# A graph network of two layers on one core: group 1's input loaded early into a tile of another pool, and the timetable of its steps changed

## Chip, cores, metric

One core of one Trainium2 chip. The metric is the device time of one execution in microseconds (us); medians of several executions are quoted. All executions used here are in the fast state; the mean granted TensorE clock of the profiled ones lies between 0.988 and 0.992 of full speed.

## The reference, cut to what matters

128 graphs of 128 nodes with 256 features pass two layers. `adj` is a 128x128 matrix of integers for each graph.

```python
# layer 0: two graph attentions in a row, then a feed-forward part
Wh = h @ W;  e = leaky_relu(Wh @ a[:F] + (Wh @ a[F:]).T, 0.2)
att = softmax(where(adj > 0, e, -9e15), axis=1)
h = att @ Wh                                     # done twice (W1, a1; W2, a2)
h = layernorm(x + h)
x = layernorm(h + relu(h @ w_ff1) @ w_ff2)
# layer 1: attention with 8 heads and 4 relations, then a feed-forward part
attn = softmax(q @ k.T / sqrt(32))
out = sum over r of (attn * (adj == r)) @ (x @ Wv[r])
x = layernorm(x + out @ Wo)
x = layernorm(x + gelu(x @ W1) @ W2)
```

## The kernel before

The kernel takes four graphs as a group; there are 32 groups, counted from 0. Each of the five stages of a group (load, graph attention "gat", feed-forward 0, attention, feed-forward 1) is a Python generator. A generator emits some instructions and yields a distance. A heap merges the generators of all groups by time, so the numbers in `TIMES`, `EARLY` and `stages` are a timetable that decides in which order PE's instructions (and, by the scheduler, those of the other engines) stand. They are no waits.

```python
TIMES = {
    "sums": 5, "ff unit": 3, "ff2": 4, "ff half": 10, "row": 13, "gat": 18, "wh": 5.5,
    "gat copy": 0, "qk": 4.5, "scores": 5, "turn0": 10, "turn1": 5,
    "v0": 5.5, "mask0": 0, "av": 6.5, "v": 3.5, "mask": 3,
    "end": 1, "lead ff0": 26, "lead att": 32, "lead ff1": 32, "affine": 6, "store": 25,
}
...
def load_group(g):                                # xT and mask of a group
    xt = ld.tile([P, DC, T], F32, name="xt", bufs=1)
    nc.sync.dma_start(xt, xT[g])
    return xt, load_mask(g)
...
def unit(f0):                                     # in feed_forward: one half of the first product
    ...
    product(chain, 1, True); product(side, 5, True)            # product: L300
    nc.scalar.copy(lo[:, :, 0], chain); nc.scalar.copy(hi[:, :, 1], side)
    yield
    ...
    nc.vector.tensor_add(lo[:, :, 1], lo[:, :, 1], side)       # L315
    yield
    product(chain, 7)
    nc.vector.tensor_add(hi[:, :, 1], hi[:, :, 1], chain)      # L318
    yield
    product(chain, 4)                             # L300 again: writes the same PSUM tile, so it waits for L318
    for i in range(2):
        nc.scalar.activation(lo[:, i], lo[:, i], func, ...)    # L322
    for i in range(2):
        nc.scalar.activation(hi[:, i, 1], ...)                 # L325
        nc.scalar.activation(hi[:, i, 0], chain[:, i], ...)    # L326: gives the PSUM tile back
    yield
...
def gat_weighting(wh, c, cap, direct):            # the softmax of one graph attention
    ...                                           # not direct: the row goes out and back through DRAM
        nc.vector.transpose(z, ...)                            # L359, zs
        nc.sync.dma_start(s.rearrange(...), z[::Q])            # L361, zsd <- zs
        nc.sync.dma_start(p, ...)                              # L363, e <- zsd
    yield TIMES["row"]
    ...                                           # Prelu L366, cap L367, max L369, exp L372, 1/s L373
    nc.gpsimd.tensor_mul(e, e, per_row(s, N))                  # L374
    return e

def gat_block(direct, tag, g, xt, at):
    ...                                           # wh = x W, L385
    att = yield from gat_weighting(wh, D + 2, cap, direct)
    yield TIMES["gat"]
    ...                                           # first att @ wh, L393; copies L394
    yield TIMES["gat copy"]
    nc.sync.dma_start(y, x[g])                                 # tok
    att = yield from gat_weighting(wh, D, cap, direct)
    yield TIMES["gat"]
    ...                                           # second att @ wh, L403
...
# attention: weights(b) = scores L438, max L444, exp L448, scaling L450; turned = transpose L249 or
# through DRAM L255 to L260; by_relation = mask L464; values L471, L472; weighted = av product L483
    yield TIMES["qk"]
    es = [weights(0)]
    yield TIMES["scores"]
    es.append(weights(1))
    ...
    yield TIMES["v0"]
    v, ms = values(0), {}
    for k in range(0, 8, 2):
        by_relation(0, eT[0], ms, PARTS[k // 2:k // 2 + 1])
        yield TIMES["mask0"]
    for b in range(G):
        ...
        yield TIMES["av"]
        oT, last = weighted(ms, v)
...
stages = (stage_load, -81), (stage_gat, -39), (stage_ff0, 48), (stage_attention, 132), (stage_ff1, 300)
```

The second product after the softmax, the output projection, is L521; the second matrix of the feed-forward part is L343.

## Time and profile before

| | kernel before |
|---|---|
| time, median (range, runs) | 3256.7 us (3255.5 to 3259.5, 4) |
| profiled span | 3254.6 us |
| PE busy | 3137.8 us |
| period of a steady group | 97.9 us (start of L385 to start of L385) |
| first transposes of group 0 (L249) | 61.5 us |
| L385 of group 3, of group 4 | 198.3, 280.8 us |

How to read it: PE is nearly always busy, so only PE's order and PE's waits matter. It is best to divide the run into four parts: the **head** (to the start of L385 of group 3), the **transition** (from there to L385 of group 4, 82.5 us, where few groups are under way and PE often stands idle), the **steady groups** (groups 4 to 31, one every 97.9 us) and the **tail**. The lines are in the prediction below.

### The profile page before, as it was taken

Reading aid. Unit: us, or ns where it says so; the run is one execution under the profiler, and the core shown is the slowest. Engines: PE = TensorE matmul, PEld = TensorE weight load, DVE = VectorE, ACT = ScalarE, POOL = GpSimd, SP = SyncE. Lnnn points to the kernel's source line nnn. Section 1 sums busy time; section 2 is a strip of 40 time slices with the busy share of each in tenths; the row PEclk is TensorE's granted clock in tenths of the full one; section 3 lists DMA queues with packets and bytes.
Section 4 is the critical chain, followed back from the end, with each engine's and each line's share of the span. In section 5 each row is a group of like instructions: output and inputs, shape, how many; then the busy total and the mean of one; then the engine's idle time right before and its main releaser. Section 6 shows DMA issues by size and latency. Waiting matters only on the chain. (4 is left out here: it accounts for less than half of the span.)

```text
span 3254.6 us, 55388 instructions
## 1 busy us (share of the span) xinstructions
PE 3137.8 (96%) x20160; PEld 2371.9 (73%) x20160; DVE 2025.8 (62%) x3647; ACT 1761.5 (54%) x5191; POOL 1379.6 (42%) x1736
## 2 busy tenths in 40 slices
PE   6989999999999999999999999999999999999988
PEld 5756777777777777777777777777777777777766
DVE  2566576566576566576566666566666566666563
ACT  3545555565555565555565555565555565555443
POOL 2324445344345344345344345344344443354342
PEclk8999999999999999999999999999999999999999
DMA  4244453544454444454544454544454544453310
GB/s 151 62 107 98 98 120 91 115 94 101 99 119 97 110 93 96 104 118 92 117 92 98 104 114 95 117 91 98 103 116 94 117 85 102 104 115 86 86 33 14
DMA packets 1156401, 320.84 MB, mean 99 GB/s; under 512 B 902944, under 2 KB 1126688, under 8 KB 1156000
## 3 DMA queue, kind: packets, MB, share of 16 engines
q1 hardware_dynamic: 1156128, 317.29, 43.1%
q8 instruction: 160, 2.62, 0.3%
q14 instruction: 113, 0.93, 0.1%
HBM read 187.58 MB, written 129.62 MB: 97 GB/s over the span
## 5 line engine op out<-in xcount | busy, mean ns | idle before, releaser
L464 DVE SCALAR_TENSOR_TENSOR m<-adj,eT 128x1024 f32<-128x1024 f32 x512 | 596.4, 1211 | 170.8 <-DMA eT<-zd 168.3
L238 POOL TENSOR_TENSOR tok<-tok,ln_rows 128x512 f32<-128x512 f32 (+1 forms) x636 | 666.9, 1061 | 70.8 <-ACT tok L232 36.5
L450 POOL TENSOR_TENSOR e<-e,s 128x512 f32<-128x512 f32 x256 | 265.0, 1040 | 524.3 <-DVE s L449 394.1
L343 PE MATMUL mm<-wf,fT 128*128 128x256 f32 x2048 | 456.9, 381 | 26.5 <-ACT e L448 26.5
L471 PE MATMUL mm<-wv,T 128*128 128x512 f32 x1024 | 464.3, 596 | 0.6 <-ACT e L448 0.6
L343 PE MATMUL mm<-w,fT 128*128 128x256 f32 x2048 | 455.5, 381 | 0.0
L343 PEld LDWEIGHTS mm<-wf,fT 128*128 128x128 f32 x2048 | 387.2, 190 | 91.0 <-ACT e L448 37.8
L448 ACT ACTIVATE e<-mm,nm 128x128 f32<-128x128 f32 x1024 | 360.5, 377 | 167.0 <-DVE nm L444 141.1
L343 PEld LDWEIGHTS mm<-w,fT 128*128 128x128 f32 x2048 | 387.5, 190 | 73.3 <-issue 24.2
L232 ACT ACTIVATE tok<-tok,nmr,rstd 128x256 f32<-128x256 f32 x512 | 263.3, 597 | 137.8 <-POOL nmr L230 125.3
L471 PEld LDWEIGHTS mm<-wv,T 128*128 128x128 f32 x1024 | 191.9, 190 | 199.9 <-issue 184.4
L344 DVE TENSOR_TENSOR tok<-tok,mm 128x512 f32<-128x512 f32 x128 | 88.0, 687 | 380.7 <-PE mm L343 369.2
L374 POOL TENSOR_TENSOR e<-e,s 128x512 f32<-128x512 f32 x64 | 67.0, 1048 | 492.6 <-DVE s L373 371.9
L483 PE MATMUL av<-m,v 128*32 128x128 f32 x8192 | 255.2, 277 | 17.4 <-DVE m L464 13.3
L483 PEld LDWEIGHTS av<-m,v 128*32 128x32 f32 x8192 | 219.5, 111 | 62.7 <-issue 45.9
L276 POOL TENSOR_TENSOR t<-T 128x256 f32<-128x256 f32 x64 | 46.7, 730 | 499.3 <-DMA T<-zd 498.8
L426 ACT ACTIVATE kbd<-mm,col 32x512 f32<-32x512 f32 x256 | 173.7, 679 | 151.6 <-PE mm L423 147.5
L444 DVE TENSOR_REDUCE nm<-mm 128x4 f32<-128x512 f32 x256 | 163.3, 677 | 125.2 <-PE mm L438 125.2
L448 ACT ACTIVATION_READ_ACCUMULATOR e<-mm,nm 128x1 f32 x1024 | 222.1, 217 | 0.0
L472 DVE TENSOR_TENSOR v<-mm,bv 128x512 f32<-128x512 f32 x256 | 169.5, 683 | 50.4 <-PE mm L471 50.4
L300 PE MATMUL mm<-T,w 128*128 128x256 f32 x768 | 197.3, 387 | 0.2 <-ACT T L253 0.2
L487 ACT COPY oT<-av 128x256 f32<-128x256 f32 x128 | 48.3, 378 | 270.1 <-PE av L483 270.1
(121 smaller groups left out, 5230.4 us busy)
## 6 DMA issues: line engine op xcount, KB each, us to landing
zd<-e SPq DMA_DIRECT2D x496, 128.0 KB, 3.4
eT<-zd SPq DMA_DIRECT2D x124, 512.0 KB, 4.0
zd<-T SPq DMA_DIRECT2D x364, 128.0 KB, 3.0
T<-zd SPq DMA_DIRECT2D x91, 512.0 KB, 3.8
xt<-in_xT_dram SPq DMA_DIRECT2D x32, 512.0 KB, 5.0
at<-in_adjT_dram SPq DMA_DIRECT2D x64, 256.0 KB, 5.3
tok<-in_x_dram SPq DMA_DIRECT2D x32, 512.0 KB
out_dram<-tok SPq DMA_DIRECT2D x31, 512.0 KB, 6.2
```

What stands on the lines that cost most here:

```text
L232: nc.scalar.activation(y[:, b], y[:, b], AF.Identity, bias=nmr[:, b:b + 1], scale=rstd[:, b:b + 1])
L238: engine.tensor_tensor(y[:, b:b + n], y[:, b:b + n], v[:, None, :].to_broadcast([P, n, D]), op)
L300: nc.tensor.matmul(p[:, i], win[k][:, ts(f0 + i, P)], hs[k], start=first and i == 0, stop=True, skip_group_check=True)
L343: nc.tensor.matmul(p[:, b - b2_], fT[f][:, ts(b, N)], wout[:, f], start=n == 0, stop=n == FC - 1)
L426: nc.scalar.activation(kbd[c][rows, :, q % 2], p[rows], AF.Identity, bias=bk[rows, c:c + 1])
L444: nc.vector.tensor_reduce(nm, p, AX.X, OP.max, negate=True)
L448: nc.scalar.activation(eh[:, q], p[:, q], AF.Exp, bias=nm[:, q:q + 1], accum_out=s[:, q:q + 1])
L450: nc.gpsimd.tensor_mul(eh, eh, per_row(s, N))
L464: nc.vector.scalar_tensor_tensor(m, ab, r, eT, op0=OP.is_equal, op1=OP.mult)
L471: nc.tensor.matmul(p, hT[:, b, f], wv[:, f, r:r + 2], start=f == 0, stop=f == DC - 1)
L472: nc.vector.tensor_add(v[:, r:r + 2].rearrange("p r d -> p (r d)"), p.rearrange("p r d -> p (r d)"), bv[:, r * D:(r + 2) * D])
L483: last = nc.tensor.matmul(po[ts(q, DH), c], v[:, r, c * P + q * DH:c * P + (q + 1) * DH], ms[r][:, q // 2 * HC + c * 2 + q % 2], start=r = ...
```

## The change

Its intent: xT of group 1 and its mask are loaded with the first loads, into a buffer of the pool of the T tiles, which is free at that time, so group 1 needs not wait for group 0's xT buffer. The distances around the two products of graph attention (gat, gat copy), between the first two scores, of the last affine, and the start of the loads change the timetable.

```diff
-    "sums": 5, "ff unit": 3, "ff2": 4, "ff half": 10, "row": 13, "gat": 18, "wh": 5.5,
-    "gat copy": 0, "qk": 4.5, "scores": 5, "turn0": 10, "turn1": 5,
+    "sums": 5, "ff unit": 3, "ff2": 4, "ff half": 10, "row": 13, "gat": 16, "wh": 5.5,
+    "gat copy": 2, "qk": 4.5, "scores": 5.5, "turn0": 10, "turn1": 5,
...
-    "end": 1, "lead ff0": 26, "lead att": 32, "lead ff1": 32, "affine": 6,
+    "end": 1, "lead ff0": 26, "lead att": 32, "lead ff1": 32, "affine": 7,
...
-    (1, 0): 49, (1, 1): 78, (1, 2): 48, (1, 3): 0, (1, 4): 0,
+    (1, 1): 78, (1, 2): 48, (1, 3): 0, (1, 4): 0,
...
+    second_xt = wk.tile([P, G * MW], F32, name="xt1", tag="T", bufs=TB)[:, :DC * T].rearrange("p (c t) -> p c t", c=DC)
+    nc.sync.dma_start(second_xt, xT[1])
+    second_at = load_mask(1)
...
+    loads[1] = second_xt, second_at
...
-        if g > 0:
+        if g > 1:
             loads[g] = load_group(g)
...
-    stages = (stage_load, -81), (stage_gat, -39), (stage_ff0, 48), (stage_attention, 132), (stage_ff1, 300)
+    stages = (stage_load, -75), (stage_gat, -39), (stage_ff0, 48), (stage_attention, 132), (stage_ff1, 300)
```

From here on, a line of the changed kernel has a number 3 or 4 higher than the same line of the kernel before: L303 is L300, L321 is L318, L329 is L326, L346 is L343, L377 is L374, L388 is L385, L396 is L393, L406 is L403, L441 is L438, L451 is L448, L467 is L464, L475 is L472, L486 is L483, L524 is L521 (L525 in the runs that add a line).

## The prediction

> **What bounds the kernel now.** I read the page first, then PE's busy time by stretch, PE's waits, and its timeline in three places. Line numbers are those of the kernel before.
>
> ```profile
> PE 3137.8 (96%) x20160; PEld 2371.9 (73%) x20160; DVE 2025.8 (62%) x3647; ACT 1761.5 (54%) x5191; POOL 1379.6 (42%) x1736
> ```
>
> PE is busy for 96% of a span of 3254.6 us; DVE, next, for 62%. The change adds no matmul, so it can only win some of the 117 us in which PE stands idle. Where these lie is in the busy time by stretch (columns: stretch, its length, then busy us of PE, PEld, DVE, ACT, POOL, then clock, DMA share, GB/s):
>
> ```profile
> 25.00:50.00 25.00, 9.97 (x35) 7.67 (x35) 5.27 (x11) 11.14 (x45) 2.08 (x2) 0.75 0.44 160
> ...
> 75.00:200.00 125.00, 124.44 (x716) 95.79 (x715) 78.54 (x139) 60.76 (x175) 41.08 (x50) 1.00 0.35 79
> ...
> 250.00:275.00 25.00, 20.32 (x132) 15.79 (x131) 18.07 (x32) 12.08 (x37) 12.57 (x15) 0.86 0.65 152
> ...
> 300.00:3100.00 2800.00, 2753.28 (x17864) 2082.29 (x17857) 1799.12 (x3242) 1563.30 (x4632) 1240.19 (x1557) 1.00 0.46 102
> ```
>
> Length less PE's busy time gives 6.2 us idle in 0 to 25, 15.0 in 25 to 50, 7.2 in 50 to 75, 0.6 in 75 to 200, 21.1 in 200 to 275, 46.7 in 300 to 3100 (28 groups of four graphs, one each 97.9 us, so 1.67 us a group), and 20.4 after that. PE's waits from 300 to 3000 name two (us in total, times, longest):
>
> ```profile
> PE mm L343 <- ACT e L448: 26.5, 28, 0.9
> PE mm L300 <- DVE fT L318: 17.3, 28, 1.0
> ```
>
> **The head**, PE's timeline (start, us, idle before in brackets):
>
> ```profile
> 35.10 6.51 PE L385 MATMUL mm<-wx,xt 128*128 128x260 f32 x16 [9.63 <-DMA xt<-in_xT_dram]
> ...
> 41.56 1.04 PE L393 MATMUL mm<-wh,e 128*128 128x258 f32 x4
> ...
> 49.71 3.81 PE L393 MATMUL mm<-wh,e 128*128 128x258 f32 x8 [5.24 <-POOL e L374]
> 53.31 0.42 PE L356 MATMUL mm<-ident,wh 128*128 128x128 f32 x1
> 53.52 2.31 PE L403 MATMUL mm<-wh,e 128*128 128x256 f32 x8
> ```
>
> Group 1's first matmuls (L385, 35.10) wait for its xT, which was issued last of all loads. Group 0's L393 stands behind them: its weights were scaled on POOL by 31.17, yet it starts at 41.56. Then group 1's L393 (49.71) stands ahead of group 0's L403, whose weights were ready at 49.66. So group 0, whose chain sets the whole beginning, pays for group 1 twice.
>
> **The steady groups**, one example, PE and ACT:
>
> ```profile
> 1597.02 1.96 PE L300 MATMUL mm<-t,wf 128*128 128x256 f32 x8 [0.57 <-DVE fT L318]
> 1598.92 1.95 PE L483 MATMUL av<-m,v 128*32 128x128 f32 x64
> 1600.80 1.13 PE L438 MATMUL mm<-kbd,T 64*128 64x256 f32 x8
> 1601.87 2.47 PE L393 MATMUL mm<-wh,e 128*128 128x258 f32 x8
> ...
> 1605.28 0.92 PE L343 MATMUL mm<-wf,fT 128*128 128x256 f32 x3 [0.94 <-ACT e L448]
> ```
>
> L343 needs a PSUM buffer. The built program deals the six "mm" buffers out in rotation; L393 takes four after the scores (L438) take two, so L343 gets the one that the first half of the scores still fills until four exponentials (L448, 1603.72 to 1605.23) have read it. L393 itself is stretched (2.47 us against about 1.75 for eight passes in a row): two of its four buffers were held by a feed-forward until L326 (ACT, 1602.04 to 1603.58).
>
> **What the Trainium skill says.** "TensorE: Matmul & The Clock Gate", Part 3, The mechanism: matmuls run strictly first in, first out. The trace agrees: L393 with its data ready at 31.17 waited for the L385 ahead of it to 41.56. Same page, Part 1: after some 3.4 us idle the array runs at half clock until it has been busy about as long. The trace agrees in kind: passes of 260 columns take about 0.40 us at 18 to 24 and 35 to 41 us and 0.22 in the steady part; the slow spell lasts about 6 us here. "PSUM — Partial Sum Buffer", Specifications: 8 banks of 2 KiB a partition. The program agrees: six mm, one adj, one av, so no seventh buffer can be added. No page bears on the scheduler's timetable.
>
> **Part 1: xT of group 1 (and its mask) loaded sixth and seventh, into a T buffer.** 0.77 MB go ahead of col and wf1, at the 0.37 MB/us that the DMA moved then: 2.1 us. wf1 landed at 11.2, PE was free for it at 11.8; now it lands at 13.3, so PE loses about 1.5 us. From there, by durations of the trace: L182 7 us (to 20.3), L385 of group 0 6.4 (26.7), L385 of group 1 at once and mostly at full clock 3.5 (30.2). In the built program ACT and PE now take both groups in step: L366 of both, then L372 of both. L366 of group 0 ends about 32, DVE's L367 and L369 (0.69 each) 33.3, L372 (four, 1.7 us) 35.1, L373 and L374 (1.0) 36.5. L393 of group 0 at 36.5, not 41.6; of group 1 at about 40, not 49.7. Copies end near 43.2, L366 of both 45.6, L372 47.7, POOL 49.0: L403 of group 0 at about 49.1, not 53.5. Half of the gain goes in the lock-step and in a cold clock (3.4 us for L403, not 2.3). The transposes of L249, at 61.47 before, come about 4 us sooner. From 75 to 200 PE is full and its order is unchanged, so the 4 us pass through. **About -4 us.**
>
> **Part 2: L393 and L403 of the third group, 200 to 275.** With "gat" 16, "gat copy" 2 and "scores" 5.5, L393 now stands before the av product instead of after the scores, and L403 before L521. The lines that matter:
>
> ```profile
> 232.42 3.31 PE L483 MATMUL av<-m,v 128*32 128x128 f32 x64 [12.94 <-DVE m L464]
> ...
> 236.73 2.01 PE L393 MATMUL mm<-wh,e 128*128 128x258 f32 x8
> ...
> 257.95 3.78 PE L403 MATMUL mm<-wh,e 128*128 128x256 f32 x8 [4.68 <-POOL e L374]
> ```
>
> L393's weights were ready at 224.76, so its 2.0 us fall into the 12.9 us wait. Its row then reaches the second softmax earlier and L403's 4.7 us wait goes; its 3.8 us shrink to about 1.8. The sum is 8.7. What follows is limited by masks: the next av, at 270.77 before, waits for a transpose through DRAM that the new order of DVE (four masks before two reductions) makes about 2 us later; by hand I get 262 to 263. **About -8 us.**
>
> **Part 3: the 28 steady groups.** New order on PE: L300, L393, L483, L438, L343. L393's four buffers are two long free and two that the values (L471) give back by 1598.67, so it needs no wait: 1598.75 to 1600.5. L483 to 1602.4. The scores now get the two buffers that L326 holds. ACT's L326 pairs end at 1602.8 and 1603.58 before; the new order on POOL puts one more 128x512 product (1.25 us) ahead of the second L230 and takes one 128x256 (0.73) from before the first; with L374 0.8 us earlier, the second half of L232 starts about 0.4 us later, so L326 ends at 1603.2 and 1603.96. First scores 1603.25, other half 1604.0, last 1604.85; L343 then has its buffer at once. 1605.28 less 1604.85 is 0.43 us; 28 of them 12. The 0.57 us wait for L318 stays: DVE's four masks (4.6 us) still stand in front of it in the new order. **About -12 us.** In plain words: one wait goes and most of it returns as a wait of L438 on L326.
>
> **Part 4: loads at -75 and affine 7.** The output store now goes out ahead of xT; xT is loaded some 6 us later, 20 us or more before it is read. 0. The end has the same PE order; 0.
>
> Sum: 4 + 8 + 12 = 24, so 3256 - 24 = **3232 us**, 0.7% less.
>
> **Rivals.** A: the steady wait goes entirely. For: the named wait of 26.5 us has its cause in the buffer order, which is changed; if ACT keeps its old pace or POOL's earlier L374 speeds it up, the scores start sooner. Against: L326's end was already later than the new start of the scores (1602.4). Then the steady part gives 0.9 us and more a group, 26 us, and the time is 3218. B: the wait moves in full to L438, or DVE, whose zs transpose now waits for ACT's copies before it may reduce the scores, delays masks too. For: ACT and DVE run in order. Against: the masks have over 10 us of slack before the next av. Steady 0, time 3244. C: the head gains nothing, because PE works cold longer and the weights land later: 3236. D: a load or store blocks the one DMA queue and holds a transpose each group: over 3256; the store waits on the final affine, but it was ready in all but two groups of the trace before.
>
> **Range and chances.** A and B span 3218 to 3244 with the head as worked; head and transition may each be off by 4. I take 3212 to 3249. 2% faster would be 3191: 65 us, over half of all idle time and more than all named waits between 300 and 3000; 2% slower needs 2.3 us new wait in each group, and PE's only new neighbours have slack. Faster 0.03, same 0.96, slower 0.01.
>
> **What would show it.** Right: PE's busy time unchanged near 3135; L343 no longer waits on L448 in the steady part, and L438 waits on L326 instead, some 0.4 to 1.5 us a group; L300 on L318 still 28 times about 0.6; period about 97.45; L249 of group 0 near 57.5; the wait of 4.7 us on L374 near 258 gone. Wrong: no wait of L438 and a period under 97.1 (A); a period of 97.9 (B); L249 at 61 (C); PE waiting on masks or on DMA in the steady part (D).

## The result, and the profile after

| | before | after |
|---|---|---|
| time, median (range, 4 runs each) | 3256.7 us | 3241.6 us (3239.7 to 3242.8) |
| ratio of fast runs | | 0.9952 (95%: 0.9935 to 0.9969) |
| profiled span | 3254.6 us | 3241.0 us |
| period of a steady group | 97.9 us | 97.5 us |

A ratio is the mean time of one kernel's fast runs over that of the other's in the same rounds, so it is not quite the ratio of the medians quoted. The kernel before took 3256.87, 3257.75 and 3259.34 us (medians) in the three later sessions; ratios are always within a session.

The page's line of busy times, in the changed kernel:

```profile
PE 3145.3 (97%) x20160; PEld 2383.3 (74%) x20160; DVE 2020.5 (62%) x3647; ACT 1766.8 (55%) x5191; POOL 1378.8 (43%) x1736
```

PE's busy time rose by 7.5 us with the same matmuls. Some of what was idle time now stands inside instructions; the runs below show how much that hides.

**Head.** L396 of group 0 starts at 35.98 us, L406 at 48.91, and the first transposes, in the kernel before (L249) and in the changed one (L252), as PE's timeline shows (start, us, idle before in brackets):

```profile
61.47 1.67 PE L249 MATMUL mm<-ident,tok 128*128 128x128 f32 x6 [5.31 <-ACT tok L232]
57.05 1.67 PE L252 MATMUL mm<-ident,tok 128*128 128x128 f32 x6 [4.36 <-ACT tok L235]
```

Predicted were 36.5, 49.1 and 57.5. The shift against the kernel before is 4.4 us at L252 and still 3.9 us at 110 us. There it falls to 2.5 us within 2 us, and 2.7 us reach L388 of group 3 (195.7, not 198.3). The reason is the clock, here in PE's busy time by stretch (stretch, length, busy us of PE, PEld, DVE, ACT, POOL, then clock, DMA share, GB/s):

```profile
106.00:108.00 2.00, 2.00 (x13) 2.00 (x13) 1.58 (x2) 0.37 (x3) 1.36 (x2) 0.56 0.00 0
108.00:110.00 2.00, 2.00 (x9) 1.77 (x8) 1.97 (x4) 0.57 (x1) 2.00 (x3) 0.58 0.00 0
```

PE was busy throughout, at little over half the clock; in the kernel before the clock stayed at 1.00 there. The first eight transposes of this stretch (L252) took 1.95 us, and 1.07 in the kernel before. Just before came 32 matmuls of one column each (L185, folding an offset into a bias).

**Transition**, PE's waits from 200 to 300 us (us, times, longest), and the queue of the engine SP (start, us it took to issue):

```profile
PE mm L396 <- POOL e L377: 5.3, 1, 5.3
PE mm L406 <- POOL e L377: 4.3, 1, 4.3
PE av L486 <- DVE m L467: 3.8, 1, 3.8
PE av L486 <- DVE v L475: 2.6, 1, 2.6
```

```profile
230.88 2.66 SPq L261 DMA_DIRECT2D zd<-T  x4
237.35 0.38 SPq L263 DMA_DIRECT2D T<-zd  x1
...
238.39 0.54 SPq L364 DMA_DIRECT2D zsd<-zs  x1
```

The wait of 12.9 us on the masks became one of 5.3 on L396's weights and one of 3.8 on the masks, but L406 still waits 4.3 us. Its row was transposed on DVE by 231.04, but its way out (L364) was issued only at 238.39: the queue first had to issue T<-zd, which reads what zd<-T writes and so waited for that to land, to 237.35. The Trainium skill says why it must wait ("DMA: Bandwidth & Descriptors", Two DMAs through the same engine are not ordered: the issuing engine is to wait on the first transfer's semaphore before it issues the dependent one). The trace agrees, and shows the price: what stood behind in the same queue waited 3.8 us with it (zd<-T was issued by 233.54, T<-zd at 237.35).

The transition took 81.4 us (195.7 to 277.1), against 82.5. Matmul for matmul, the lead over the kernel before grows from 2.7 us at its start to 5.4 at the values after the moved L396 (L474 at 234.04, L471 at 239.39 before): that move wins 2.7. The lead is still 5.0 us after L406 and falls to 3.7 at the end, where L303 waits 1.5 us on L321.

**Steady groups**, PE's waits from 300 to 3000, then an example:

```profile
PE mm L303 <- DVE fT L321: 16.7, 28, 0.9
PE mm L441 <- ACT fT L329: 12.6, 27, 0.5
```

```profile
1588.12 1.96 PE L303 MATMUL mm<-t,wf 128*128 128x256 f32 x8 [0.57 <-DVE fT L321]
1589.93 1.90 PE L396 MATMUL mm<-wh,e 128*128 128x258 f32 x8
1591.76 1.95 PE L486 MATMUL av<-m,v 128*32 128x128 f32 x64
1594.18 1.85 PE L441 MATMUL mm<-kbd,T 64*128 64x256 f32 x8 [0.47 <-ACT fT L329]
1595.96 7.17 PE L346 MATMUL mm<-wf,fT 128*128 128x256 f32 x32
```

The wait of 26.5 us on the exponentials is gone; half of it came back as L441's wait on L329. Note that L441's eight scores take 1.85 us here and took 1.13 before.

### The profile page after: what moved, and what is told of

Read it like the earlier page. It is cut to its first block, busy times and chain, and to the rows that moved or that the text cites. A ratio compares the mean times of both kernels' runs of the same rounds, so it can differ in the third digit from the quotient of the medians.

```text
span 3241.0 us, 55392 instructions
## 1 busy us (share of the span) xinstructions
PE 3145.3 (97%) x20160; PEld 2383.3 (74%) x20160; DVE 2020.5 (62%) x3647; ACT 1766.8 (55%) x5191; POOL 1378.8 (43%) x1736
## 4 chain that ended last, share of the span: by engine, by line
PE 75%; POOL 9%; ACT 7%; DVE 6%; DMA 1%; issue 1%; SPq 1%; ACTq 0%; POOLq 0%; DVEq 0%
PE mm L346 28%; PE mm L303 13%; PE mm L474 10%; PE av L486 5%; POOL tok L241 5%; PE mm L441 5%; PE mm L388 3%; PE mm L420 3%; PE mm L426 3%; PE mm L524 3%; ACT fT L325 2%; ACT tok L235 2%; POOL rstd L232 2%; PE mm L406 2%; DVE st L226 1%; ACT fT L328 1%
## 5 line engine op out<-in xcount | busy, mean ns | idle before, releaser
L467 DVE SCALAR_TENSOR_TENSOR m<-adj,eT 128x1024 f32<-128x1024 f32 x512 | 598.8, 1213 | 228.5 <-DMA eT<-zd 161.9
L451 ACT ACTIVATE e<-mm,nm 128x128 f32<-128x128 f32 x1024 | 360.7, 376 | 190.0 <-DVE nm L447 167.2
L474 PE MATMUL mm<-wv,T 128*128 128x512 f32 x1024 | 464.2, 596 | 0.0
L346 PE MATMUL mm<-wf,fT 128*128 128x256 f32 x2048 | 456.9, 381 | 0.0
L346 PE MATMUL mm<-w,fT 128*128 128x256 f32 x2048 | 455.5, 381 | 0.2 <-DVE v L475 0.2
L346 PEld LDWEIGHTS mm<-w,fT 128*128 128x128 f32 x2048 | 386.6, 190 | 74.6 <-issue 23.8
L346 PEld LDWEIGHTS mm<-wf,fT 128*128 128x128 f32 x2048 | 386.4, 190 | 63.3 <-ACT wh L397 9.3
L235 ACT ACTIVATE tok<-tok,nmr,rstd 128x256 f32<-128x256 f32 x512 | 269.4, 594 | 178.7 <-POOL nmr L233 166.2
L474 PEld LDWEIGHTS mm<-wv,T 128*128 128x128 f32 x1024 | 191.5, 190 | 199.6 <-issue 189.3
L486 PE MATMUL av<-m,v 128*32 128x128 f32 x8192 | 254.8, 276 | 8.8 <-DVE v L475 4.9
L486 PEld LDWEIGHTS av<-m,v 128*32 128x32 f32 x8192 | 218.8, 111 | 54.3 <-issue 41.6
L377 POOL TENSOR_TENSOR e<-e,s 128x512 f32<-128x512 f32 x64 | 66.5, 1039 | 432.7 <-DVE s L376 338.4
L451 ACT ACTIVATION_READ_ACCUMULATOR e<-mm,nm 128x1 f32 x1024 | 219.8, 215 | 0.0
L303 PE MATMUL mm<-T,w 128*128 128x256 f32 x768 | 197.0, 386 | 0.2 <-ACT T L256 0.2
L475 DVE TENSOR_TENSOR v<-mm,bv 128x512 f32<-128x512 f32 x256 | 167.5, 684 | 46.8 <-PE mm L474 46.8
L303 PE MATMUL mm<-T,wf 128*128 128x256 f32 x768 | 192.6, 380 | 0.0
```

Source lines behind the costliest of these rows:

```text
L235: nc.scalar.activation(y[:, b], y[:, b], AF.Identity, bias=nmr[:, b:b + 1], scale=rstd[:, b:b + 1])
L303: nc.tensor.matmul(p[:, i], win[k][:, ts(f0 + i, P)], hs[k], start=first and i == 0, stop=True, skip_group_check=True)
L346: nc.tensor.matmul(p[:, b - b2_], fT[f][:, ts(b, N)], wout[:, f], start=n == 0, stop=n == FC - 1)
L451: nc.scalar.activation(eh[:, q], p[:, q], AF.Exp, bias=nm[:, q:q + 1], accum_out=s[:, q:q + 1])
L467: nc.vector.scalar_tensor_tensor(m, ab, r, eT, op0=OP.is_equal, op1=OP.mult)
L474: nc.tensor.matmul(p, hT[:, b, f], wv[:, f, r:r + 2], start=f == 0, stop=f == DC - 1)
```

## The experiments

Where each run gained or lost is read from its profile by the starts of L388 (L385) of group 3, of group 4 and of the last group's second half, and by the end of the last matmul, each less that of the kernel before (us). A single execution's head can differ by a microsecond or two: spq, for one, begins group 3 2.3 us before the changed kernel.

| run | group 3 | group 4 | transition took | last group | end | period |
|---|---|---|---|---|---|---|
| before | 0 | 0 | 82.5 | 0 | 0 | 97.9 |
| changed | -2.7 | -3.7 | 81.4 | -14.4 | -13.1 | 97.5 |
| times | -1.0 | 2.1 | 85.5 | -8.3 | -7.3 | 97.5 |
| head | -2.8 | -2.8 | 82.4 | -0.9 | 1.5 | 97.9 |
| sc5 | -3.6 | -1.2 | 84.8 | -1.2 | -2.3 | 97.9 |
| spq | -4.9 | -3.9 | 83.5 | -14.9 | -15.1 | 97.5 |
| mk3 | -2.4 | -3.0 | 81.9 | -61.6 | -61.3 | 95.7 |
| elo | -4.1 | -5.7 | 80.9 | -48.1 | -48.9 | 96.3 |
| dir0 | 9.0 | 9.0 | 82.5 | -0.9 | 0.4 | 97.5 |
| bmk3 | 0.4 | 0.8 | 82.9 | -33.7 | -33.0 | 96.6 |
| elomk3 | -5.1 | -4.3 | 83.2 | -68.1 | -68.7 | 95.5 |
| elomk3dir0 | 10.1 | 9.2 | 81.5 | -54.6 | -54.0 | 95.5 |
| spqelomk3 | -3.9 | -2.3 | 84.0 | -67.4 | -66.6 | 95.5 |
| wide | -5.9 | -0.3 | 88.1 | -10.9 | -9.8 | 97.5 |

All runs were correct.

### The timetable alone (times)

```diff
 # the changed kernel, less the early load
+    (1, 0): 49, (1, 1): 78, ...
-    second_xt = ...; nc.sync.dma_start(second_xt, xT[1]); second_at = load_mask(1)
-        if g > 1:
+        if g > 0:
```

> The kernel before with all the timetable's numbers of the change, but group 1's xT loaded where it was. Theory (head and steady part are separate gains): the steady part and the transition come with it, the head does not: period 97.5 us, L252 of group 0 (first transposes) near 61.5 us as before, time 3244 to 3246 (that of the kernel before less 11 to 12). Rival (the distances do nothing until group 0 is no longer held by group 1's load): 3255 and a period of 97.9.

Measured: 3248.78 us, ratio 0.9973 (0.9963 to 0.9984). The period is 97.5 us, so the steady gain comes from the timetable alone, and the rival falls. The head is as before within a microsecond (L249 at 60.5). But the transition took 3 us more than before, with an av product that waited 9.9 us for DVE's values; that was not foreseen.

### The early load alone (head)

```diff
 # the changed kernel with the old numbers
-    ... "gat": 16, "gat copy": 2, "scores": 5.5, "affine": 7;  (stage_load, -75)
+    ... "gat": 18, "gat copy": 0, "scores": 5, "affine": 6;  (stage_load, -81)
```

> The kernel before with only the early second xT (and its place in the timetable), all other numbers as before. Theory: first transposes near 57.5 us, so a shift of 4 us, of which 2.5 to 4 are left at the end: 3252 to 3254; period 97.9 with L343's wait on L448 as before. The drop of the shift from 3.9 to 2.5 us near 110 us, where the granted clock fell in the changed kernel's profile, should show here too if the earlier start causes it, and not if it was an accident of that execution. Rival (the head's gain is given back by 300 us): 3256.

Measured: 3256.00 us, ratio 0.9998 (0.9990 to 1.0006). The first transposes came at 57.1 us, 2.8 us were left at L388 of groups 3 and 4, and then they melted: steady groups a few hundredths of a microsecond longer, a last one 0.9 longer, and a tail in which the transposes waited 6.0 us on POOL (2.2 before). The drop of the clock came here too, with L252 taking 1.95 us. So the load by itself is worth nothing in the end, which is the rival's time, though by another way: in this profile the head's gain was given back after 300 us, more than half of it in the tail. The profiled execution was 1.9 us slower than the run's median, so where exactly the gain goes is not settled.

### The scores' distance back (sc5)

```diff
-    "gat copy": 2, "qk": 4.5, "scores": 5.5, ...
+    "gat copy": 2, "qk": 4.5, "scores": 5, ...
```

> The changed kernel with the scores' distance back at 5: L396 goes back behind the scores in every group, nothing else of PE's order moves. Theory (the steady gain is this one move): the wait of L346 on the exponentials L451, some 0.9 us in 28 groups, is back, that of L441 on L329 is gone, period 97.9, time 3251 to 3254. Rival (the move of L406 ahead of L524, which stays here, or the POOL order, makes the gain): period below 97.7 and time under 3248.

Measured: 3254.44 us, ratio 0.9993 (0.9987 to 1.0000). PE's waits from 300 to 3000:

```profile
PE mm L346 <- ACT e L451: 26.2, 28, 0.9
```

The old wait is back, none of L441 on L329 is left, the period is 97.9 us: the steady gain is the move of L396 ahead of the scores. It needs "scores" and the pair "gat" and "gat copy" together: in the built programs, "gat" 18 and "gat copy" 0 also put L396 back, and "scores" 5.5 alone in the kernel before does not move it.

### The row ahead in the queue (spq)

```diff
+    (0, 4): -4, (1, 1): 78, ...
-        yield TIMES["lead ff0" if before == "01" else "lead ff1"]
+        yield TIMES["lead ff0" if before == "01" else "lead ff1"] - lead    # 4 for ff1 of group 0, else 0
```

> The changed kernel with the feed-forward of group 0 a little later for the DMA queue and its lead 4 shorter, so that in the transition the SP queue issues the row of group 3 (zs out, e back) ahead of group 0's transposed T; PE's order is the same. Theory (L406's wait of 4.3 us near 248 us stays because the queue issued that row only at 238 to 243 us, behind a transfer that waits for its own landing): the row starts 5 us or more sooner, the wait of L406 on L377 falls below 1 us, and the time falls by 2 to 4 us against the changed kernel: 3238 to 3240. Rival (masks and T sums set the transition, and the wait on the row only stood beside theirs): the wait goes but another of 3 to 4 us on DVE L467 or POOL L280 comes, and the time stays within 1 us of 3241.6.

Measured: 3242.88 us, ratio 0.9954 (0.9941 to 0.9966), the same as the changed kernel's 0.9952. The queue and PE's waits from 200 to 300 us:

```profile
227.60 0.53 SPq L364 DMA_DIRECT2D zsd<-zs  x1
...
231.57 4.67 SPq L261 DMA_DIRECT2D zd<-T  x4
```

```profile
PE av L486 <- DVE m L467: 3.5, 1, 3.5
PE mm L303 <- DVE tok L407: 2.6, 1, 2.6
PE mm L303 <- DVE fT L321: 2.2, 1, 2.2
```

The row was issued 11 us sooner, and L406's wait is gone: it started at 247.67, not 252.12 (2.3 of these 4.4 us this execution had already at L388 of group 3, where the clock had not fallen). Yet L388 of group 4 starts at 276.9 against 277.1. L303 waits 2.6 us on DVE's L407, which stands behind four masks, which waited for eT to come back from DRAM (DVE L467 at 251.38, idle 1.96 before it); later L303 waits 2.2 on L321, and the last matmuls run on a cold clock (0.57 from 274 to 278 us). The reason for L406's wait is shown; that taking it away in this manner wins time is refuted. The rival holds.

### The first graph's masks 3 later (mk3)

```diff
         v, ms = values(0), {}
+        yield 3
         for k in range(0, 8, 2):
             by_relation(0, eT[0], ms, PARTS[k // 2:k // 2 + 1])
...
-            yield TIMES["av"]
+            yield TIMES["av"] - (0 if b else 3)
```

> The changed kernel with the first graph's four masks of each group emitted 3 later in the timetable (and the first av product's distance 3 shorter, so PE's order is the same). DVE then takes the sums L318 and the first L321 ahead of the masks, and ACT takes the first activations L325 in the gap before the second half of L235. Theory (of the two waits left in a steady group, L303 on L321 comes from the four masks, 4.6 us, standing ahead of it on DVE, and L441 on L329 from ACT beginning its activations late): both waits go, 0.6 and 0.45 us a group, period 96.5 to 96.8, time 3241.6 less 20 to 29, so 3213 to 3222. Rival (the two waits are one slack: take the first away and L441 waits so much longer for L329): period 97.5, time 3240 to 3243.

Measured: **3191.89 us**, ratio 0.9797 (0.9784 to 0.9810): 50 us less than the changed kernel, where the two named waits add up to 29.3 (16.7 and 12.6). PE has no wait on L321 or L329 left. Excerpts, first DVE and ACT of the changed kernel:

```profile
1582.18 4.61 DVE L467 SCALAR_TENSOR_TENSOR m<-adj,eT 128x1024 f32<-128x1024 f32 x4
...
1587.30 1.28 DVE L321 TENSOR_TENSOR fT<-fT,mm 128x512 f32<-128x512 f32 x2
```

```profile
1587.29 2.08 ACT L235 ACTIVATE tok<-tok,nmr,rstd 128x256 f32<-128x256 f32 x4 [1.69 <-POOL nmr L233]
1589.27 1.32 ACT L325 ACTIVATE fT<-fT,col 128x512 f32<-128x512 f32 x2
...
1593.31 1.54 ACT L329 ACTIVATE fT<-mm,col 128x256 f32<-128x256 f32 x4
```

Then DVE and ACT of this run, in the same part of a group, which lies elsewhere in time here:

```profile
1561.25 0.69 DVE L321 TENSOR_TENSOR fT<-fT,mm 128x512 f32<-128x512 f32 x1
1561.85 2.35 DVE L467 SCALAR_TENSOR_TENSOR m<-adj,eT 128x1024 f32<-128x1024 f32 x2
```

```profile
1563.47 1.32 ACT L325 ACTIVATE fT<-fT,col 128x512 f32<-128x512 f32 x2
...
1565.49 2.06 ACT L235 ACTIVATE tok<-tok,nmr,rstd 128x256 f32<-128x256 f32 x4
```

DVE takes L321 ahead of the masks, and ACT fills the 1.7 us in which it stood idle. The mechanism is that of the theory, the size is not: the period is 95.7, not 96.5 to 96.8. Counted from start to start (mean of 25 groups), the part from L474 to L346 takes 12.02 us in the changed kernel and 10.22 here, 1.79 less, which is 50 us in 28 groups. Of this, 0.76 lies ahead of L303 (named as a wait of 0.6), 0.52 ahead of L441 (named as 0.45) and 0.47 inside L441's eight scores, where no wait is named. The next run tells what that is.

### The activations of lo one step earlier (elo)

```diff
             product(chain, 7)
             nc.vector.tensor_add(hi[:, :, 1], hi[:, :, 1], chain)
+            for i in range(2):
+                nc.scalar.activation(lo[:, i], lo[:, i], func, bias=bin_[:, f0 + i:f0 + i + 1])
             yield
             product(chain, 4)
-            for i in range(2):
-                nc.scalar.activation(lo[:, i], lo[:, i], func, bias=bin_[:, f0 + i:f0 + i + 1])
```

> The changed kernel with the two activations of lo (L325) emitted one step earlier, before the last product of the feed-forward's chain; PE's and DVE's orders are the same. ACT then takes half of L325 into its idle time before L235. Theory (the wait of L441, new with the change, is for a PSUM buffer that L329 gives back, and L329 is late because of what ACT has ahead of it): the wait of L441 on L329 (0.45 us, 27 or 28 times) goes, period 97.0 to 97.1, time 3241.6 less 11 to 12.5. L303's wait on L321 stays. Rival (L346 or the exponentials take it up, as L329's other buffers are needed later): period 97.5, time unchanged.

Measured: 3208.82 us, ratio 0.9850 (0.9837 to 0.9864), period 96.3 us. Only the wait on L329 was taken away; PE's example:

```profile
1571.02 1.97 PE L303 MATMUL mm<-t,wf 128*128 128x256 f32 x8 [0.57 <-DVE fT L321]
...
1576.54 1.19 PE L441 MATMUL mm<-kbd,T 64*128 64x256 f32 x8
1577.65 7.17 PE L346 MATMUL mm<-wf,fT 128*128 128x256 f32 x32
```

From L303 to L346 it is 6.63 us, in the changed kernel 7.84: 1.21 us a group. Of these the named wait is 0.47, and L441 takes 1.19 instead of 1.85 us, which is 0.66 more. In the changed kernel the first scores waited for one buffer of L329 and the later ones for the other, and the second wait stands *inside* L441's busy time. PE's own list names 27 waits, one a group. The waits of the weight loads (PEld), from 300 to 3000, show both, 56 in the changed kernel and 4 small ones here:

```profile
PEld mm L441 <- ACT fT L329: 32.1, 56, 0.8
PEld mm L441 <- ACT fT L329: 0.8, 4, 0.2
```

The expectation counted only the first. This is why PE's busy time rose with the change. "Perfetto Trace Analysis", Identifying the Most-Contended Engine, in the Trainium skill calls matmul busy time a bad measure of the distance to the roofline and points to the weight loads' busy share. PE showed 97% here while 50 us could still be won, so the trace agrees on the first; the weight loads' share only rose from 74% to 75% with these 50 us (mk3). The page gives as reason that pipelined instructions look smaller, and here they looked larger.

### Group 0's weights transposed on PE (dir0)

```diff
-        x2[g] = yield from attention(x1.pop(g), g, g == 0, g == NG - 1)
+        x2[g] = yield from attention(x1.pop(g), g, g == 0, alone(g))        # alone: first or last group
```

> The changed kernel with group 0's attention weights transposed on PE (32 more transposes, some 4.3 us of PE) and not through DRAM. Theory, formed after the run with the queue reordered (there L406's wait of 4.3 us went and a wait of 2.6 us behind the masks and a cold clock took its place: the transition from 200 to 280 us is set by the masks, which wait for the weights' way through DRAM, some 7 to 10 us each): the masks come sooner, PE's idle time between 200 and 281 us falls from about 20 to under 13 us, and the time falls by 2 to 6 us. Rival (the transition is set by the work of DVE and ACT, which goes up here by eight copies of 0.6 us): no change or 1 to 3 us more.

Measured: 3256.01 us, ratio 0.9993 (0.9987 to 1.0000), 14 us worse than the changed kernel. The new transposes stood in the stretch that had been full, one of them waiting 7.4 us on POOL, so L388 of group 3 came 11.7 us later than in the changed kernel. The transition itself took 82.5 us. But the run does not test its theory: the edit missed the transition. In the changed kernel the queue sends group 0's weights out (zd<-e) at 146, 152, 165 and 181 us, all ahead of the transition; the four between 215 and 262 us are group 1's, and in this run they still go through DRAM:

```profile
227.99 2.66 SPq L261 DMA_DIRECT2D zd<-e  x4
...
255.41 3.32 SPq L261 DMA_DIRECT2D zd<-e  x4
```

The av product still waited 4.9 us on masks. Whether the masks, through their weights' way over DRAM, set the transition stays open.

### The three together (elomk3dir0), and without the transposes (elomk3)

> The three edits together, as a version that might beat both kernels. Theory: their gains add, as they lie in different waits, except that the masks' move and the earlier activations both serve L441's wait (0.45 us once, not twice): period 96.4 to 96.7 and 3241.6 less 25 to 34, so 3208 to 3217. Rival (a new wait, such as the av product on its masks or the values): period above 96.9, time above 3222.

Measured: 3200.67 us, ratio 0.9822 (0.9809 to 0.9836). The period is 95.5 us, below the expected 96.4 to 96.7, as L441's hidden wait goes too; but the 10 us lost ahead of the transition stay lost.

> The changed kernel with both edits that helped (masks 3 later, activations of lo one step earlier), without group 0's transposes on PE, which cost 13 us ahead of 290 us. Theory: the steady period of the run with all three (95.5 us against 95.7 with the masks alone, as L441 takes 1.13 and not 1.38 us), with the transition of the changed kernel: 3192 less 5 to 6, so 3185 to 3188. Rival (the scheduler's other order on DVE and ACT costs the transition or the tail what the period gains): 3190 to 3194.

Measured: **3187.07 us**, ratio 0.9779 (0.9764 to 0.9793), as expected: this version beats both kernels, the first by 2.2%, the changed one by 1.7% (of the medians, from different sessions). L441 takes 1.13 us in it. PE is busy for 2599.63 of the 2600 us from 300 to 2900; the idle time that the profile still shows lies ahead of and after that.

### With the queue reordered as well (spqelomk3)

> The same with the queue reordered in the transition as well. Theory from the earlier run (the wait on the row goes, other waits take its place): within 2 us of the run without it. Rival (with the masks and activations moved, the transition is no longer held by the masks): 3 to 5 us less.

Measured: 3190.48 us, ratio 0.9790 (0.9776 to 0.9805), 3.4 us more than without it, where at most 2 were expected. L406's wait of 4.9 us is gone again, and L303's wait on L321 grew from 1.7 to 4.1 us. The rival falls, and the reordered queue costs a little.

### The masks' edit on the kernel before (bmk3)

```diff
 # in the kernel before, its own timetable
+        yield 3
-            yield TIMES["av"]
+            yield TIMES["av"] - (0 if b else 3)
```

> The kernel before with the same one edit as the run with the masks emitted 3 later (PE's order is that of the kernel before). It asks whether the reordering by the change was needed for that gain of 50 us. Theory: ACT was the late engine in both kernels (in the kernel before the exponentials L448 started at 1603.72, just after L326 ended at 1603.58). With the activations earlier, the exponentials start when the reductions are done, about 1602.1, and end near 1603.6; L393 is no longer stretched and ends near 1603.05, so L343 still waits some 0.5 us for the buffer of the scores: period 96.0 to 96.4, time 3208 to 3216, so most of the gain comes without the change. Rival (the wait of L343 on L448 grows by what L393 no longer takes): period 97.3, time near 3240.

Measured: 3222.95 us, ratio 0.9891 (0.9876 to 0.9906), period 96.6. The waits on L448 and L318 are gone. A new one, from 300 to 3000:

```profile
PE av L483 <- DVE v L472: 30.2, 28, 1.1
```

The av product now waits for the values, which stand behind the masks on DVE. In the changed kernel this time is filled: L396 stands there. So the change's order is worth 0.9 us a group once the masks are moved (95.7 against 96.6), and 0.4 without that. The theory named the right main cause and missed the new wait; the rival (97.3) falls.

### The folding matmuls 64 columns wide (wide)

```diff
-            p = ps.tile([P, n], F32, name="mm")
+            p = ps.tile([P, n, 64], F32, name="mm")
-                    nc.tensor.matmul(p[:, f:f + 1], w[:, c, ts(f, P)], offset[:, c:c + 1], ...)
+                    nc.tensor.matmul(p[:, f], w[:, c, ts(f, P)], offset[:, c:c + 1].to_broadcast([P, 64]), ...)
-            nc.vector.tensor_add(bias, bias, p)
+            nc.vector.tensor_add(bias, bias, p[:, :, 0])
```

> The changed kernel with the one-column matmuls that fold an offset into a bias (L185) done 64 columns wide, so that the array streams more in the same instructions. In the changed kernel's profile the granted clock fell to 0.5 to 0.6 for 3 to 4 us right after the 32 of them near 103 to 107 us, and the head's gain of 3.9 us fell to 2.5; this happened in 7 of the 8 profiles with the early head and in neither of the two without it. Theory (a stretch of 3.6 us of one-column matmuls counts as idle for the clock): the first transposes of that stretch (L252, 8 of them) take 1.07 and not 1.95 us, the clock stays at 1.0, time 1 to 1.5 us less than 3241.6. Rival (the drop has another cause): L252 still takes 1.95 us.

Measured: 3246.34 us, ratio 0.9963 (0.9950 to 0.9975). The clock, and the transposes (L253 here):

```profile
106.00:108.00 2.00, 2.00 (x15) 1.87 (x14) 2.00 (x4) 0.76 (x2) 1.94 (x2) 1.00 0.00 0
```

```profile
105.88 1.04 PE L253 MATMUL mm<-ident,tok 128*128 128x128 f32 x8
```

The drop is gone, and L389 of group 3 started at 192.4, 3.3 us earlier than in the changed kernel. But the edit also moved some instructions in the scheduler's order, the transition then took 88.1 us with a wait of 7.7 us for the values, and the time was not better (the two ratios' intervals overlap). One profile supports the theory of the clock; it is no proof, as in the run spq the clock stayed up there with one-column matmuls (L252 at 104.8, 1.07 us). Of the ten profiles with the early head and the one-column form, nine show the drop; of the three with the later head (before, times, bmk3), none. "TensorE: Matmul & The Clock Gate", Part 1, says that activity is judged in a free-running window of about 3.4 us: the 32 matmuls last 3.63 us where the clock holds, so they would fill such a window only if it happens to begin with them. Nine in ten is a lot for such a chance, so the window alone does not explain it; no run here shows its phase, and the cause stays open.

## Why the prediction was right or wrong

The time lay in the range, 10 us above the point, and the class was right. That was not a matter of errors that cancel: after the first step all of them lie on the same side, and the width of the range took them up. By its own steps, with the profiles' numbers (medians: -15 us):

| step | predicted | measured |
|---|---|---|
| head, to L252 | -4 | -4.4 |
| 75 to 200 us, "so the 4 us pass through" | 0 | +1.8 |
| transition | -8 | -1.1 |
| 28 steady groups | -12 | -10.7 |
| tail | 0 | +1.3 |
| sum | -24 | -13.1 |

**Head: right.** Order, lock-step of both groups and cold clock came as worked out. That PE's unchanged, full order passes the gain on was wrong by 1.8 us, of which 1.4 were lost at once near 110 us: the same instructions took longer, as the clock fell to little over half. And head shows that an earlier start alone need not reach the end at all.

**Steady groups: right in mechanism and size.** L343's wait went, L438's wait on L326 came, the period is 97.5 (predicted 97.45). sc5 shows that this one move makes it, times that the early load has no part in it. The prediction had the stretched scores in its sums ("First scores 1603.25, other half 1604.0"); my expectations of the later runs forgot it, and were too low: elo won 33 us where 11 to 12.5 were expected. Rival A's reasoning (the wait goes entirely) became true only with other edits.

**Transition: the failing step.** It was "Its row then reaches the second softmax earlier and L403's 4.7 us wait goes", and from it "About -8 us". First, the wait did not go (4.3 us): the row was transposed at 230.8 to 231.0, but the one queue stood on another transfer's landing until 237.35. I had looked at PE's, ACT's and DVE's order in the built program, not at what the queue would wait for. Second, and this weighs more, spq removes exactly this wait and wins nothing: the waits of PE in the transition stand side by side with others that take their place. Four edits that move or remove a wait there (times, sc5, spq, spqelomk3) gave a transition of 83.5 to 85.5 us, against 81.4 in the changed kernel. Adding up waits (2.0 of the 12.9 filled, 4.7 gone, and 2.0 for a warmer L403) was the error; only the first term came true, with 2.7 us (L393's 2.0 and a wait of 0.65 behind it). What sets the transition's 81 us remains open; L406's wait on its row alone does not. That the masks do, through the way of group 1's weights over DRAM, no run tested, as dir0 changes group 0 only. The prediction also called the group of this step the third; it is the fourth (group 3).

**Tail: not foreseen.** Of the 1.3 us, 1.1 are lost at the eight transposes L252 at 2999.07 us: they wait for ACT's L235, 0.26 us ahead of them and within them (1.91 us, and 1.09 before, at full clock both times). L524 waits 3.7 us on L490 later, and 1.9 before, but that is caught up. The gains of one part depend on where the others leave the clock and the order: the timetable alone took 7.3 us off the profile, the load alone none, both 13.1.

The loads at -75 and the affine distance were not run by themselves. In the built programs the loads' number moves 30 transfers in the queue (26 output stores and the loads of two groups) and nothing else, and the affine number nothing.

## What to carry to other kernels

When PE is 97% busy, compare the duration of a group of matmuls with the same group elsewhere in the trace: eight scores of 1.85 instead of 1.13 us hid more than the wait that was named beside them, and the waits of the weight loads showed it. Removing the cause (four masks ahead of one small sum on DVE, an idle gap on ACT ahead of the activations) gave 50 us where the waits promised 29. In a stretch where many chains are short of work, do not add up waits; ask what ends last after each of them is gone, and test it. Before counting on an earlier transfer, read its queue: a transfer that waits for another's landing holds what stands behind it in the same queue (3.8 us here). And before an edit is called a test of a stretch, look in its profile whether the stretch changed: dir0's four transfers were still there.

## What the Trainium skill lacked or had wrong

- "Perfetto Trace Analysis", Identifying the Most-Contended Engine: it says that pipelined PE instructions look smaller in the trace. Here a group that waits for its second PSUM buffer looks larger, as each of its records lasts 0.38 us or more and covers the wait: L441 1.85 us against 1.13, and PE's busy time 3145 us against 3124 for the same 20160 matmuls in the run mk3.
- "TensorE: Matmul & The Clock Gate", Part 1, speaks of idle windows. It lacks that PE can be busy without a gap and still lose the clock: after 32 one-column matmuls in 3.9 us the granted clock was 0.56 to 0.58 from 106 to 110 us (such a drop in nine of ten profiles; in the run spq the one-column form kept the clock), and 64 columns wide in 3.7 us it stayed at 1.0 (one profile).
- "DMA: Bandwidth & Descriptors", Two DMAs through the same engine are not ordered, tells to wait in the issuing engine. It lacks the price: with one issuing queue a row ready at 231.0 us was sent at 238.4, 3.8 us of it for another transfer's landing.
- No page has how much an emission order is worth: the same matmuls in the same order on PE, with other orders on DVE and ACT, took 3241.6 and 3191.9 us.
